# The first image's attention biases: interpolation along x moved from VectorE and ScalarE to TensorE, with diagonals made by GpSimd

## The chip, the cores and the metric

The kernel runs on one core of a Trainium2 chip. The core's engines work side by side, each through its own list of instructions in order: TensorE (PE in the profile; PEld is its weight loading), VectorE (DVE), ScalarE (ACT), GpSimd (POOL) and SyncE (SP, which here only starts transfers). The metric is the device time of one execution in microseconds (us). The kernel before takes 4742.62 us in the median of three runs (4736.29 to 4742.63).

## The reference, cut to what matters

The program takes four images of 32 x 32 positions with 384 channels through four residual layers. The change is in layer 0, a deformable attention with 6 heads of 64 channels. Its core is, per image:

```
offset = tanh(...) * [Hq/2, Wq/2];  pos = offset + ref          # one position per key and head
k, v  = projections of x sampled bilinearly at pos
attn  = einsum('bhmn', qh, k) * scale                           # 1024 queries x 1024 keys per head
disp  = (ref[query] - pos[key]) * 0.5
bias  = bilinear_sample(rpe_table[head], disp)                  # one value per (query, key)
attn  = softmax(attn + bias, over keys)
out   = attn @ v
```

For a fixed key the displacements of all queries form a regular grid, shifted by the key's own position. So the 1024 biases of one key are a window of a (doubled) table, read at one fractional shift in y and one in x. The kernel gathers such a window for each key and interpolates it twice: between neighbouring rows (y), and then between neighbouring columns (x). The weights of both steps belong to the key, so with keys on partitions they are one number per partition.

All of it is in 32-bit floats.

## The kernel before, in words

`kernel` builds the program image by image. Layer 0 of image 0 (`Front.layer0(0)`) runs to its end before the trunk (layers 1 to 3) of image 0 begins; the layer 0 of images 1 to 3 is woven into the trunk of the image before. So only in image 0 does layer 0's attention stand by itself. It has its own routine, `heads0`; images 1 to 3 use `head0`, which the change leaves alone.

`heads0` works in blocks (h, q, j): head h (6), half q of the queries (2), tile j of 128 keys (8), 96 blocks in all. A block's logits are 128 keys (partitions) x 512 queries. Eight blocks with the same h and q are called a half here; there are 12. One call of `turn(t)` issues one step of a software pipeline that is written out by hand, with `pin` keeping the order as written on every engine. With `AHEAD, SUB, OUT = 5, 10, 11`, turn t issues, for different blocks:

- POOL: the gather of the window `win` for block t+10 (L913, ring of 6 buffers);
- DVE: the second half of the y step for block i = t+5, `z = win_below * f + z` (L925), and the second half of the x step for block t+4, `lg = z_right * f + lg` (L930);
- ACT: the first half of the x step for block t+5, `lg = z_left * f` (L935), and the first half of the y step for block t+6, `z = win * f` (L944, `z` in a ring of 4);
- PE, in even turns: the products of keys and queries for blocks t+2 and t+3, into the two halves of one PSUM tile `big` (L955; there are two such tiles);
- DVE: `lg = product + lg` for block t (L975), and the running maximum over the key tiles, `rmax` (L980);
- at the end of a half, PE transposes `rmax` (L985), DVE reduces it (L966), POOL makes a diagonal of the maxima (L970), PE spreads it over all partitions by a product with ones (L1010), and ACT copies it to `tb` (L989);
- for block t-10: DVE subtracts `tb` (L994) and ACT takes the exponential (L995);
- for block t-11: PE multiplies by the values and, in the other half of its columns, by ones for the denominators (L1004, both accumulate over the eight blocks);
- after a half, ACT copies the outputs over the queries in `qpad` (L1019) and the row of denominators to a buffer (L1024) that SP sends to DRAM; `divide` fetches reciprocals back and scales the outputs (L905).

`lg` is a ring of 20 buffers of 128 x 512; two of them serve `divide` as `inv` from time to time. Beside the turns, `early0` (norm of image 1: transposes L560 and L583, group sums L338, their copies on ACT and statistics on DVE) is advanced by one step per turn. After the last turn comes the output projection (L388), which needs the scaled outputs of the last heads.

In PSUM, a block's result comes from two recorded passes of one product: the 96 products of L955 are 192 records.

Of the kernel before, what the change touches and what calls it, by code (L numbers as in the profile page):

```python
# [21 lines left out]
ALU = mybir.AluOpType  # L22
# [388 lines left out]
class Front(Lane):  # L411
# [447 lines left out]
    def heads0(self, work):  # L859

        nc, v, pin = self.nc, self.nc.vector, self.tc.keep_in_program_order
        f, va = self.f, self.va
        HH, HN = HW // 2, N // 2
# [1 line left out]
        blocks = [(h, q, j) for h in range(G) for q in range(2) for j in range(NJ)]  # L867
        n = len(blocks)

        AHEAD, SUB, OUT = 5, 10, 11  # L870
        win, z, lg, ps, half, dens, inv = {}, {}, {}, {}, {}, {}, {}

        def tile_of(shape, tag, bufs):
            return work.tile(shape, F32, tag=tag, name=self.nm(tag), bufs=bufs)
# [8 lines left out]
        def divide(step, k):  # L883
            heads = (2 * k, 2 * k + 1)
            by_row = lambda a: a.rearrange("o (p i) -> (o p) i", p=P)
            if step == 0:
                dens[k] = tile_of([P, 2, NJ], "dens", 2)
                for r, h in enumerate(heads):
                    nc.sync.dma_start(dens[k][:, r, :], by_row(self.den[h]))
            elif step == 1:  # L890
                pin(v.reciprocal(dens[k], dens[k]))
                for r, h in enumerate(heads):
                    nc.sync.dma_start(by_row(self.rden[h]), dens[k][:, r, :])
                for q in range(2):
                    inv[q] = tile_of([P, HN], "lg", 20)
                    for r, h in enumerate(heads):
                        nc.sync.dma_start(
                            inv[q][r * GC : (r + 1) * GC],
                            self.rden[h][0, q * HN : (q + 1) * HN].partition_broadcast(GC),
                        )  # L900
            else:
                for q in range(2):
                    out = queries(2 * k, q)
                    w = inv[q].rearrange("p (y x) -> p y x", x=HW)
                    pin(v.tensor_tensor(out, out, w, ALU.mult))  # L905

        def turn(t):
            i = t + AHEAD

            if i + 5 < n:  # L910
                h, q, j = blocks[i + 5]
                win[i + 5] = tile_of([P, (HH + 1) * WROW], "win", 6)
                nc.gpsimd.indirect_dma_start(  # L913
                    out=win[i + 5],
                    out_offset=None,
                    in_=self.strips[:, :],
                    in_offset=bass.IndirectOffsetOnAxis(
                        ap=self.widx[:, q, j * G + h : j * G + h + 1], axis=0
                    ),
                )  # L920
            at = lambda i: blocks[i][2] * G + blocks[i][0]
            sc = lambda i, axis, side: f[:, side, axis, at(i) : at(i) + 1]
            if 0 <= i < n:
                wv = win.pop(i).rearrange("p (r c) -> p r c", c=WROW)
                pin(v.scalar_tensor_tensor(  # L925
                    z[i], wv[:, 1 : HH + 1, 0 : HW + 1], sc(i, 1, 0), z[i], ALU.mult, ALU.add
                ))
            if 0 <= i - 1 < n:
                zi, lf = z.pop(i - 1), lg[i - 1].rearrange("p (y x) -> p y x", x=HW)
                pin(v.scalar_tensor_tensor(  # L930
                    lf, zi[:, :, 1 : HW + 1], sc(i - 1, 0, 0), lf, ALU.mult, ALU.add
                ))
            if 0 <= i < n:
                lg[i] = tile_of([P, HN], "lg", 20)
                pin(nc.scalar.activation(  # L935
                    lg[i].rearrange("p (y x) -> p y x", x=HW),
                    z[i][:, :, 0:HW],
                    AF.Copy,
                    scale=sc(i, 0, 1),
                ))  # L940
            if 0 <= i + 1 < n:
                wv = win[i + 1].rearrange("p (r c) -> p r c", c=WROW)
                z[i + 1] = tile_of([P, HH, HW + 1], "z", 4)
                pin(nc.scalar.activation(  # L944
                    z[i + 1], wv[:, 0:HH, 0 : HW + 1], AF.Copy, scale=sc(i + 1, 1, 1)
                ))

            if t >= -2 and (t + 2) % 16 == 0 and t + 18 < n and t + 2 >= 16:
                self.load_keys(blocks[t + 18][0])
            if t >= -2 and t % 2 == 0 and t + 2 < n:  # L950
                big = self.big()
                for u in range(2):
                    h, q, j = blocks[t + 2 + u]
                    ps[t + 2 + u] = big[:, u * 512 : (u + 1) * 512]
                    pin(nc.tensor.matmul(  # L955
                        ps[t + 2 + u],
                        self.kz[h % 2][:, j * P : (j + 1) * P],
                        queries(h, q),
                        start=True,
                        stop=True,  # L960
                    ))

            m = (t - 1) // NJ
            if t > 0 and t % NJ == 0 and t <= n:
                top = tile_of([P, NI], "top", 2)
                pin(v.tensor_reduce(  # L966
                    top, half[m, "t"].rearrange("p (i n) -> p i n", i=NI), AX.X, ALU.max
                ))
                diag = tile_of([P, NI, P], "diag", 1)
                pin(nc.gpsimd.tensor_tensor(  # L970
                    diag, bc(self.ident, 1, NI), bc(top, 2, P), ALU.mult
                ))
            if 0 <= t < n:
                m, j = divmod(t, NJ)
                pin(v.tensor_tensor(lg[t], ps.pop(t), lg[t], ALU.add))  # L975
                if j == 0:
                    half[m] = tile_of([P, HN], "rmax", 2)
                else:
                    first = lg[t - 1] if j == 1 else half[m]
                    pin(v.tensor_tensor(half[m], first, lg[t], ALU.max))  # L980
                if j == NJ - 1:
                    half[m, "t"] = self.bank()
                    for i in range(NI):
                        cols = slice(i * P, (i + 1) * P)
                        pin(nc.tensor.transpose(half[m, "t"][:, cols], half[m][:, cols], self.ident))  # L985
            if t > 1 and t % NJ == 1 and t <= n + 1:
                m = (t - 2) // NJ
                half[m, "b"] = tile_of([P, HN], "tb", 2)
                pin(nc.scalar.copy(half[m, "b"], half[m, "p"]))  # L989

            s = t - SUB
            if 0 <= s < n:
                tb = half[s // NJ, "b"]
                pin(v.tensor_tensor(lg[s], lg[s], tb, ALU.subtract))  # L994
                pin(nc.scalar.activation(lg[s], lg[s], AF.Exp))  # L995

            o = t - OUT
            if 0 <= o < n:
                h, q, j = blocks[o]
                if j == 0:  # L1000
                    half[o // NJ, "o"] = self.bank()
                po = half[o // NJ, "o"]
                for own, w in ((True, va[:, j, h * GC : (h + 1) * GC]), (False, self.ones[:, 0:GC])):
                    pin(nc.tensor.matmul(  # L1004
                        po[rows(h, own), :], w, lg[o], start=j == 0, stop=j == NJ - 1
                    ))
            if t > 0 and t % NJ == 0 and t <= n:
                m = (t - 1) // NJ
                half[m, "p"] = self.bank()
                pin(nc.tensor.matmul(  # L1010
                    half[m, "p"], self.ones, diag.rearrange("p i n -> p (i n)"),
                    start=True, stop=True,
                ))

            o = t - OUT - 1
            if 0 <= o < n and o % NJ == NJ - 1:
                h, q, j = blocks[o]
                po, own = half[o // NJ, "o"], rows(h, True)
                pin(nc.scalar.copy(  # L1019
                    queries(h, q)[own], po[own, :].rearrange("p (y x) -> p y x", y=HH)  # L1020
                ))
                o0 = rows(h, False).start
                den = lg[o][o0 : o0 + 1, :]
                pin(nc.scalar.copy(den, po[o0 : o0 + 1, :]))  # L1024
                nc.sync.dma_start(self.den[h][:, q * HN : (q + 1) * HN], den)

            o = t - OUT - 2
            for step, late in enumerate((0, 4, 9)):
                if o >= late and (o - late) % (4 * NJ) == 4 * NJ - 1:
                    divide(step, (o - late) // (4 * NJ))  # L1030
# [818 lines left out]
```

## Time and profile before

| | |
|---|---|
| median of the runs shown | 4742.62 us (4736.29 to 4742.63) |
| the profiled execution: its own time | 4731.65 us |
| the profiled execution: span of its instructions | 4729.8 us |
| mean granted TensorE clock | 0.926 |
| PE busy, of the whole span | 4165.4 us (88%) |
| DVE, ACT, POOL busy | 3133.8, 2416.1, 945.7 us |
| the stage of `heads0`: from the first product of keys and queries to the end of the last product with the values | 214.7 to 557.5 us of the span |

The page gives shares over the whole span, which has stages with different limits. For this change the stage from 214.7 to 557.5 us counts, and it is read with the same views limited to that window: busy time of each engine in stretches, groups of instructions by line, and the instructions in order of time. In a group, the number after x counts instructions, then come the busy time together (us) and the mean duration of one (ns); after the second bar stands how long the engine had been idle before them and what ended that. PE records overlap each other (a pass starts before the one ahead of it has drained), so a pass is priced by the distance between starts, not by its duration.

### The profile page before, as it was taken

To read this page: it belongs to the slowest core of one execution; us is meant where nothing else is said; L and a number is where in the kernel's file an instruction comes from. 1 tells how busy PE (TensorE), PEld (TensorE's weight loads), DVE (VectorE), ACT (ScalarE), POOL (GpSimd) and SP (SyncE) were. 2 spreads that over 40 slices of the span, in tenths; PEclk is the share of its full clock that TensorE was granted. 3 is DMA by queue.
4 is the path that set the end of the run, shared out by engine and by line. 5 is a ranking of instruction groups with operands and counts; after the bars stand their busy time and mean duration, and the time that the engine had idled before them with its cause. 6 is when DMAs were issued, how large, how long until landed. Compare 5 with 4: busy or idle time off the path is not lost. (4 is left out here: it accounts for less than half of the span.)

```text
span 4729.8 us, 46690 instructions
## 1 busy us (share of the span) xinstructions
PE 4165.4 (88%) x15704; PEld 1776.1 (38%) x15704; DVE 3133.8 (66%) x5772; ACT 2416.1 (51%) x3711; POOL 945.7 (20%) x946
## 2 busy tenths in 40 slices
PE   5477788999999988899899989899999999999988
PEld 2222233333333353333333444343333335343444
DVE  3599755777878727577877754767686874555544
ACT  2166433666666313566766332456675641556542
POOL 0533204221212103311212110421121211000000
PEclk8688888999999988999999989899999998999998
DMA  6435224221212143321212124431121213311011
GB/s 124 133 118 144 75 92 126 88 61 52 72 41 66 65 137 128 109 60 48 82 50 68 46 88 126 138 100 57 30 77 43 74 41 118 96 32 24 19 40 40
DMA packets 231727, 369.97 MB, mean 78 GB/s; under 512 B 117507, under 2 KB 164704, under 8 KB 231488
## 3 DMA queue, kind: packets, MB, share of 16 engines
q1 hardware_dynamic: 170472, 200.51, 14.3%
q0 software_dynamic: 39936, 145.53, 10.1%
q10 hardware_dynamic: 21080, 20.96, 1.8%
q8 instruction: 124, 2.03, 0.2%
q14 instruction: 115, 0.94, 0.1%
HBM read 287.41 MB, written 79.78 MB: 78 GB/s over the span
## 5 line engine op out<-in xcount | busy, mean ns | idle before, releaser
L1472 DVE SCALAR_TENSOR_TENSOR e<-bank,gam,e 128x512 f32<-128x512 f32 x768 | 558.4, 749 | 573.0 <-ACT gn L1471 276.8
L1463 PE MATMUL bank<-whole,sg 128*128 128x512 f32 (+3 forms) x2304 | 873.2, 513 | 2.5 <-DVE e L1472 2.5
L1323 ACT ACTIVATE big<-big,nmax 128x1024 f32<-128x1024 f32 x384 | 418.6, 1090 | 397.5 <-DVE nmax L1322 352.0
L1441 ACT ACTIVATE e<-big 128x1024 f32<-128x1024 f32 x384 | 376.9, 1019 | 360.4 <-PE big L1433 352.8
L1463 PEld LDWEIGHTS bank<-whole,sg 128*128 128x128 f32 x2304 | 406.5, 199 | 379.9 <-issue 301.7
L1322 DVE TENSOR_REDUCE nmax<-big 128x1 f32<-128x1024 f32 x384 | 453.0, 1218 | 62.0 <-PE big L1314 35.4
L792 POOL DMA_INDIRECT win<-strips,widx x288 | 307.1, 1066 | 634.0 <-DVE z L805 331.0
L1418 POOL TENSOR_SCALAR sg<-whole,gam 128x512 f32<-128x512 f32 x192 | 147.1, 769 | 1399.4 <-PE bank L1463 1139.5
L1433 PE MATMUL big<-qa,ka 64*128 64x512 f32 x1536 | 411.7, 627 | 14.7 <-ACT big L1323 8.9
L1314 PE MATMUL big<-k,q 32*128 32x512 f32 x1536 | 327.2, 690 | 74.7 <-ACT e L1441 35.3
L813 PE MATMUL bank<-qpad,kz 128*128 128x512 f32 x576 | 281.1, 614 | 15.0 <-DVE e L1472 15.0
L707 POOL DMA_INDIRECT gat<-pairs,sidx x192 | 210.0, 1094 | 418.0 <-DVE sidx L521 241.2
L848 PE MATMUL bank<-lg,va 128*64 128x512 f32 x576 | 265.4, 603 | 16.3 <-ACT lg L846 16.2
L848 PE MATMUL bank<-lg,ones 128*64 128x512 f32 x576 | 264.7, 602 | 0.0
L810 DVE SCALAR_TENSOR_TENSOR lg<-z,bias_f,lg 128x512 f32<-128x512 f32 x288 | 227.4, 802 | 39.3 <-ACT lg L809 37.1
L804 ACT ACTIVATE z<-win,bias_f 128x528 f32<-128x528 f32 x288 | 207.1, 739 | 63.1 <-DVE lg L810 40.0
L1433 PEld LDWEIGHTS big<-qa,ka 64*128 64x128 f32 x1536 | 134.7, 187 | 270.4 <-issue 153.9
L805 DVE SCALAR_TENSOR_TENSOR z<-win,bias_f,z 128x528 f32<-128x528 f32 x288 | 217.0, 772 | 27.4 <-DMA win<-strips,widx 16.4
L845 DVE TENSOR_TENSOR lg<-lg,tb 128x512 f32<-128x512 f32 x288 | 187.7, 705 | 52.3 <-ACT tb L838 51.5
L1407 PE MATMUL bank<-e,vs 128*32 128x512 f32 x1536 | 211.6, 607 | 2.1 <-DVE vs L1401 2.1
L809 ACT ACTIVATE lg<-z,bias_f 128x512 f32<-128x512 f32 x288 | 201.0, 720 | 18.3 <-PE bank L848 10.4
L814 DVE TENSOR_TENSOR lg<-bank,lg 128x512 f32<-128x512 f32 x288 | 192.4, 684 | 20.7 <-PE bank L813 18.4
(299 smaller groups left out, 6658.3 us busy)
## 6 DMA issues: line engine op xcount, KB each, us to landing
pairs<-xn SPq DMA_DIRECT2D x64, 192.0 KB
q<-qd SPq DMA_DIRECT2D x48, 256.0 KB
w<-in_gmat SPq DMA_DIRECT2D x16, 576.0 KB
w<-in_w_off SPq DMA_DIRECT2D x12, 576.0 KB
w<-in_Wqkv SPq DMA_DIRECT2D x12, 576.0 KB
a<-in_x SPq DMA_DIRECT2D x16, 384.0 KB
x<-a ACTq DMA_DIRECT2D x4, 1536.0 KB
win<-strips,widx POOLq DMA_INDIRECT x384
```

The source lines that it names most:

```text
L792: nc.gpsimd.indirect_dma_start(out=win, out_offset=None, in_=self.strips[:, :], in_offset=bass.IndirectOffsetOnAxis(ap=self.widx[:, q, c : ...
L805: v.scalar_tensor_tensor(z, wv[:, 1 : HH + 1, 0 : HW + 1], sc(0, 1), z, ALU.mult, ALU.add)
L810: v.scalar_tensor_tensor(lg, z[:, :, 1 : HW + 1], sc(0, 0), lg, ALU.mult, ALU.add)
L813: nc.tensor.matmul(ps, kz[:, j * P : (j + 1) * P], both, start=True, stop=True)
L848: nc.tensor.matmul(po[out, :], w, lf, start=j == 0, stop=j == NJ - 1)
L1314: nc.tensor.matmul(ps[r][:, h * 512 : (h + 1) * 512], self.q4[rows, i * P : (i + 1) * P], self.k4[rows, 0:512], start=True, stop=True,)
L1322: v.tensor_reduce(nmax[:, r, i : i + 1], ps[r], AX.X, ALU.max, negate=True)
L1323: nc.scalar.activation(ps[r], ps[r], AF.Exp, bias=nmax[:, r, i : i + 1], accum_out=den[:, r, i : i + 1],)
L1433: nc.tensor.matmul(ps[:, r, :], ka[rows, j * P : (j + 1) * P], qa[rows, cols], start=True, stop=True,)
L1441: nc.scalar.activation(e, ps, AF.Exp)
L1463: nc.tensor.matmul(ps[:, (mid - i0) * P :], sg[:, r, m, :], sim[:, r, m, mid * P : i1 * P], start=m == 0, stop=m == 1,)
L1472: v.scalar_tensor_tensor(e[:, r, :], ps, self.gam[:, 1:2], e[:, r, :], ALU.add, ALU.mult, accum_out=tot[:, r, h : h + 1],)
```

## The change

In `heads0` alone, the x step and the addition of the logits leave DVE and ACT:

- L930 (x step, second half), L935 (x step, first half) and L975 (adding the product) are gone.
- POOL makes, for each block, `dg`: the identity times the key's two x weights, two diagonals of 128 x 128 side by side (ring of 5).
- PE makes a block's logits in PSUM from three products in place of one: diagonal times left columns of `z`, diagonal times right columns of `z`, keys times queries.
- ACT copies the finished logits from PSUM to `lg`; DVE takes the running maximum directly from PSUM.
- `z` has 7 buffers in place of 4, `lg` 15 in place of 20, and the denominators' row is put in the half's `tb` in place of an `lg` buffer.

```diff
-        AHEAD, SUB, OUT = 5, 10, 11
+        AHEAD, SUB, OUT, LG = 5, 10, 11, 15
...
-            if 0 <= i - 1 < n:
-                zi, lf = z.pop(i - 1), lg[i - 1].rearrange("p (y x) -> p y x", x=HW)
-                pin(v.scalar_tensor_tensor(
-                    lf, zi[:, :, 1 : HW + 1], sc(i - 1, 0, 0), lf, ALU.mult, ALU.add
-                ))
             if 0 <= i < n:
-                lg[i] = tile_of([P, HN], "lg", 20)
-                pin(nc.scalar.activation(
-                    lg[i].rearrange("p (y x) -> p y x", x=HW),
-                    z[i][:, :, 0:HW],
-                    AF.Copy,
-                    scale=sc(i, 0, 1),
+                dg[i] = tile_of([P, 2, P], "dg", 5)
+                pin(nc.gpsimd.tensor_tensor(
+                    dg[i],
+                    bc(self.ident, 1, 2),
+                    bc(f[:, :, 0, at(i) : at(i) + 1].rearrange("p s o -> p (s o)"), 2, P),
+                    ALU.mult,
                 ))
...
-                z[i + 1] = tile_of([P, HH, HW + 1], "z", 4)
+                z[i + 1] = tile_of([P, HH, HW + 1], "z", 7)
...
-                    pin(nc.tensor.matmul(
-                        ps[t + 2 + u],
-                        self.kz[h % 2][:, j * P : (j + 1) * P],
-                        queries(h, q),
-                        start=True,
-                        stop=True,
-                    ))
+                    zi, di = z.pop(t + 2 + u), dg.pop(t + 2 + u)
+                    terms = (
+                        (di[:, 1, :], zi[:, :, 0:HW]),
+                        (di[:, 0, :], zi[:, :, 1 : HW + 1]),
+                        (self.kz[h % 2][:, j * P : (j + 1) * P], queries(h, q)),
+                    )
+                    for k, (w, a) in enumerate(terms):
+                        pin(nc.tensor.matmul(ps[t + 2 + u], w, a, start=k == 0, stop=k == 2))
...
-                pin(v.tensor_tensor(lg[t], ps.pop(t), lg[t], ALU.add))
+                lg[t] = tile_of([P, HN], "lg", LG)
+                pin(nc.scalar.copy(lg[t], ps[t]))
...
-                    pin(v.tensor_tensor(half[m], first, lg[t], ALU.max))
+                    pin(v.tensor_tensor(half[m], first, ps[t], ALU.max))
...
-                den = lg[o][o0 : o0 + 1, :]
+                den = half[o // NJ, "b"][o0 : o0 + 1, :]
```

More of the change, by code (lines that the diff above doesn't have):

```diff
@@ L868, in heads0 @@
         n = len(blocks)
-        AHEAD, SUB, OUT = 5, 10, 11
-        win, z, lg, ps, half, dens, inv = {}, {}, {}, {}, {}, {}, {}
+        AHEAD, SUB, OUT, LG = 5, 10, 11, 15
+        win, z, dg, lg, ps, half, dens, inv = {}, {}, {}, {}, {}, {}, {}, {}
         def tile_of(shape, tag, bufs):
@@ L894, in divide @@
                 for q in range(2):
-                    inv[q] = tile_of([P, HN], "lg", 20)
+                    inv[q] = tile_of([P, HN], "lg", LG)
                     for r, h in enumerate(heads):
```

## The prediction

> **What bounds the kernel now.** I looked first for the place of the changed lines: the groups by line put all of L913 to L1024 between 183 and 558 us. Nothing else of weight stands beside this stage, as the next one cannot begin without its outputs, so what it gains or loses the whole time does. Next I took the busy time of each engine in that window, in three plain halves of it, and in three later stretches where PE is dense. Columns: length, then busy us (instructions) of PE, PEld, DVE, ACT and POOL, granted clock, DMA share, GB/s.
>
> ```profile
> 214.70:557.50 342.80, 260.11 (x732) 84.78 (x730) 325.25 (x501) 212.86 (x337) 119.79 (x100) 0.85 0.39 117
> 415.70:442.40 26.70, 21.12 (x59) 6.22 (x56) 26.46 (x41) 17.30 (x28) 10.79 (x10) 0.88 0.34 104
> 442.40:469.10 26.70, 19.36 (x52) 5.75 (x54) 26.46 (x42) 17.51 (x28) 10.79 (x10) 0.89 0.31 95
> 600.00:700.00 100.00, 95.71 (x410) 39.63 (x410) 51.88 (x85) 33.18 (x50) 0.00 (x0) 0.96 0.25 76
> 1200.00:1400.00 200.00, 190.49 (x768) 75.64 (x765) 148.10 (x284) 125.24 (x202) 34.53 (x37) 0.97 0.16 49
> 4400.00:4500.00 100.00, 94.69 (x442) 40.34 (x441) 56.45 (x130) 60.68 (x93) 6.89 (x10) 1.00 0.09 23
> ```
>
> DVE is busy for 26.46 of a half's 26.70 us: it bounds the stage. But PE is second, at 21 of 27 us, and its figure is swollen by a clock of 0.85. DVE in order of time shows one turn:
>
> ```profile
> 447.52 0.69 DVE L994 TENSOR_TENSOR lg<-lg,tb 128x512 f32<-128x512 f32 x1
> 448.12 0.77 DVE L925 SCALAR_TENSOR_TENSOR z<-win,bias_f,z 128x528 f32<-128x528 f32 x1
> 448.80 0.75 DVE L930 SCALAR_TENSOR_TENSOR lg<-z,bias_f,lg 128x512 f32<-128x512 f32 x1
> 449.46 0.69 DVE L975 TENSOR_TENSOR lg<-big,lg 128x512 f32<-128x512 f32 x1
> 450.19 0.69 DVE L980 TENSOR_TENSOR rmax<-rmax,lg 128x512 f32<-128x512 f32 x1
> 450.79 0.68 DVE L994 TENSOR_TENSOR lg<-lg,tb 128x512 f32<-128x512 f32 x1
> ```
>
> From L994 to L994 are 3.27 us without a gap; eight turns and the reduction (0.6) make the 26.7. The change adds work to PE, so its prices come from PE in order of time, where it runs without a stop:
>
> ```profile
> 440.69 0.63 PE L985 MATMUL bank<-ident,rmax 128*128 128x128 f32 x4 [3.05 <-DVE rmax L980]
> 441.25 0.64 PE L1004 MATMUL bank<-lg,va 128*64 128x512 f32 x1
> ...
> 442.26 1.99 PE L955 MATMUL big<-qpad,kz 128*128 128x512 f32 x4
> 444.18 0.64 PE L1004 MATMUL bank<-lg,va 128*64 128x512 f32 x1
> ...
> 445.19 1.13 PE L1010 MATMUL bank<-diag,ones 128*128 128x512 f32 x2
> 446.24 0.64 PE L1004 MATMUL bank<-lg,va 128*64 128x512 f32 x1
> ...
> 658.63 5.32 PE L388 MATMUL big<-whole,w 128*128 128x512 f32 x12
> 663.78 1.02 PE L1160 MATMUL bank<-whole,w 128*128 128x512 f32 x2
> ```
>
> Twelve passes of 512 columns take 658.63 to 663.78, 5.15 us: 0.43 each. A group between others of another shape costs 0.20 more (L955: 442.26 to 444.18 is 1.92, four passes are 1.72). A block's products with the values take 1.01 us (441.25 to 442.26; the two column halves run together), two blocks in a row 4 x 0.43 + 0.15 = 1.87. The transposes take 0.56, the product with ones 1.05.
>
> **The change part by part.** *DVE.* L930 and L975 go: by starts 0.66 and 0.73 us a turn, so a turn falls to 1.9 and a half to 15.8 us. The maximum now reads PSUM; L975, which does so, has 683 ns against L980's 690: nothing. What is new is POOL beside it: while the present diagonal L970 runs, L994 takes 1.33 us at 443.60 instead of 0.69. If each `dg` costs DVE its whole length, 0.55 us, a half is 20.2.
>
> *ACT.* L935 (722 ns) goes, a copy from PSUM comes; L989 is the same copy, 586 ns. A half falls from 17.4 to about 16.3 us.
>
> *POOL.* Gather 1.21 us a block as now, and `dg`, 128 x 256. L970 is the same operation at twice the size, 1.08 us, so 0.55 by size; 1.42, the longest L970, is the upper end. A half is 8 x 1.76 + 1.08 = 15.2 us, at the upper end 22.1.
>
> *PE.* Two blocks now need 12 passes in one group, 12 x 0.43 + 0.20 = 5.36 us, and 1.87 for the values: 7.23. A half is 4 x 7.23, transposes 0.56, ones 1.05 and 0.15 for the values' group that the transposes split: 30.7 us. That is more than the 26.7 that a half takes now, and more than any other engine's new half. **PE becomes the bound.**
>
> *The stage's sum on PE.* 48 pairs x 7.23 = 347.0; 12 half ends x 1.76 = 21.1; the other PE work of the window (L560 4.2, L583 4.2, L388 3.8, L338 2.8 and 1.6, L402 0.5) 17.1. Together 385.2 us against the present 342.8: **+42.4**. Added: 2 us at the end, when PE has only two blocks' values left while the last `tb`, subtraction and exponential pass (0.58 + 0.68 + 0.63), and 2 us for some passes below full clock. **+46 us.**
>
> *Which clock.* This is the largest doubt, since the stage's own row says 0.85, the dense stretches 0.96 to 1.00. At 0.85 the sum would be 385.2 / 0.85 = 453, +110. I take the dense rows, because the new stage is dense: its start (L402, back to back until 214.7) already is, and no wait of PE is left in a half. The Trainium skill ("TensorE: Matmul & The Clock Gate", Part 1) has the gate the same way round: the array runs at half rate after an idle window of about 3.4 us and at full rate while kept busy. By it the sum is 385 and the 0.85 is the price of today's waits, such as the 3.05 us before L985 above.
>
> *Waits that the change adds.* A filling of `big` now waits for `z` (DVE), `dg` (POOL), and for maximum and copy of the blocks that held the buffer (DVE and ACT, formerly DVE alone); behind it on PE are the values' products. From the moment a pair's logits stand, DVE needs 0.6 + 0.6 + 0.7 + 0.6 and a `dg`'s 0.55 until the second maximum, about 3.1 us; PE meanwhile does values, the other buffer's filling and values, 9.1 us. That leaves 6 us. `z` is made three turns ahead. `dg` of block t+5 waits on POOL until PE has read block t's; behind it is the next gather, then due four turns later, 14.5 us (now 13.1), and no wait on a gather shows in this stage. The skill ("SBUF — State Buffer", two separate sides) speaks against giving POOL this work: a DVE operation with two SBUF inputs and a POOL operation exclude each other for their whole length. L994's 1.33 agrees. By it DVE's half is the 20.2 above, without it 15.8; neither is the bound.
>
> *What costs nothing, and its cover.* The present waits of L955 on L1019 (12.9 us on PE) vanish, as the diagonals' products come first in a filling; they lie under DVE now. Rings: an `lg` buffer is read by PE two to four turns before its reuse, ahead in PE's own order. The denominators' row in `tb` must be sent before the next-but-one half's copy, six turns or 22 us later; the transfers of this row and back at 557.5 to 563 take 2 us each. If those covers fail, a turn is lost, about 4 us per half or 48.
>
> **The rivals.** *PE waits, or stays off full clock* (+62 to +110): PE at 0.93 gives 414, +73 with the end; at 0.85 +110; a wait of 3 us per half, +36 more. For it: today's 0.85. Against: six us of slack at every filling.
>
> *PE near its floor* (+10 to +30): no 0.2 for a change of group and other work absorbed: 48 x 16 x 0.43 + 12 x 1.61 + 13 = 362.6, +20. For it: L388's even 0.43. Against: every change of shape in the lines above shows the extra.
>
> *Faster*: DVE stays the bound and its half of 15.8 to 20.2 counts, at most 12 x (26.7 - 20.2), 78 us less. The place is the filling: PE's half must be under 26.7, so (26.7 - 1.76 - 1.4) / 64 = 0.37 us a pass. No row shows less than 0.42. *No change to measure* (within 10 us) needs 0.39.
>
> *POOL the bound*: for 30.7 us a half, each `dg` would have to take 2.5 us, more than twice L970 at double the size; I count it under the first.
>
> **How the numbers follow.** PE dense, +30 to +62: 0.66. Waits or clock: 0.16. Floor: 0.11. Within 0.2% (9.5 us, about what a measurement can tell from no change): 0.03. Faster: 0.04. So faster 0.04, same 0.03, slower 0.93. The profiled execution would go from 4731.65 to about 4778. It ran 11 us under the median of the runs, which I take as the base: 4742.62 + 46, **4788 us**. The range goes from +20 (the floor) to +80 (clock near 0.91): 4762 to 4823.
>
> **What the new profile would show.** The reductions at the half ends stand 30 to 31.5 us apart in place of 26.7. In a half PE is busy nearly throughout with a clock of 0.95 or more, and DVE falls to 16 to 20 us. Fillings start 5.4 us before the next group, and the waits before them are gone. The maxima and the copies wait for PE. L994 and L925 often take over 1 us, beside `dg`. The prediction is wrong if fillings wait for `dg`, if the clock stays at 0.85, or if passes stand closer than 0.43.

## The result, and the profile after

The changed kernel takes 4780.97 us (median of four runs, 4778.16 to 4782.36) against 4739.45 (4736.17 to 4742.63): a ratio of 1.0090 with a 95% interval of 1.0077 to 1.0103, 41.5 us slower. The forecast was +46, at 4788. The profiled execution took 4779.59 us, its span is 4777.8.

The view of busy time in stretches, for the stage (first filling of `big` to the end of the last product with the values) and for two plain halves in it. Columns: length, busy us (instructions) of PE, PEld, DVE, ACT, POOL, granted clock, DMA share, GB/s.

```profile
217.30:598.80 381.50, 379.39 (x1116) 144.87 (x1115) 225.22 (x310) 192.36 (x335) 180.22 (x193) 1.00 0.35 105
434.80:465.60 30.80, 30.80 (x88) 11.24 (x88) 18.77 (x24) 15.69 (x28) 18.34 (x19) 1.00 0.38 106
465.60:496.40 30.80, 30.80 (x88) 11.23 (x88) 19.61 (x24) 15.76 (x28) 15.56 (x17) 1.00 0.28 82
```

PE is busy for 379.39 of 381.50 us at a clock of 1.00; in the two halves it never stops. DVE fell from 26.46 to 19 us a half. A half takes 30.80 us where it took 26.70. The stage is 38.7 us longer (381.5 against 342.8) and in this execution began 2.6 us later; what follows it took 4179.1 us in place of 4172.4, which is taken for the scatter between executions, since the same code stands there (the second profile of the changed kernel, in experiment 7, has 4174.1).

PE in order of time, one pair of blocks:

```profile
458.49 1.98 PE L958 MATMUL big<-z,dg 128*128 128x512 f32 x4
460.31 1.02 PE L958 MATMUL big<-qpad,kz 128*128 128x512 f32 x2
461.17 1.88 PE L958 MATMUL big<-z,dg 128*128 128x512 f32 x4
```

Four passes with the diagonals take 458.49 to 460.31, 1.82 us with the 0.1 of a group's start, two with the keys 0.86 (460.31 to 461.17): 0.43 a pass, strided `z` or not.

Groups by line in the stage (count | busy us, mean ns | idle before it and what ended that), first two of the kernel before, then those of the changed one:

```profile
L955 PE MATMUL big<-qpad,kz 128*128 128x512 f32 x192 | 118.0, 747 | 25.8 <-ACT qpad L1019 12.9 <-DVE lg L975 12.7
L925 DVE SCALAR_TENSOR_TENSOR z<-win,bias_f,z 128x528 f32<-128x528 f32 x94 | 72.0, 766 | 3.1 <-ACT z L944 3.1
```

```profile
L958 PE MATMUL big<-z,dg 128*128 128x512 f32 x384 | 183.8, 601 | 0.0
L958 PE MATMUL big<-qpad,kz 128*128 128x512 f32 x192 | 98.1, 592 | 0.0
L931 POOL TENSOR_TENSOR dg<-ident,bias_f 128x256 f32<-128x256 f32 x93 | 73.1, 786 | 7.7 <-PE big L958 6.0
L926 DVE SCALAR_TENSOR_TENSOR z<-win,bias_f,z 128x528 f32<-128x528 f32 x94 | 92.4, 986 | 6.5 <-ACT z L940 6.5
L978 DVE TENSOR_TENSOR rmax<-rmax,big 128x512 f32<-128x512 f32 x72 | 49.3, 685 | 110.9 <-ACT lg L973 110.9
```

No filling waits (0.0 idle before either group). The products with the keys, 747 ns each before, are down to 592, since no pass of a filling runs below full clock (none takes over 0.70 us). The y step on DVE grew from 766 to 986 ns beside GpSimd's diagonals, and a diagonal took 786 ns where 550 had been taken. The last line is one that nobody expected: the maximum waits for ScalarE's copy of the same block, 110.9 us in all. Both only read `big` (but for the second block of a half, whose maximum takes the copy too), so by the data alone most maxima need not wait; why the program orders them so was not tested.

### The profile page after: what moved, and what is told of

It is laid out like the page before. It is cut to its first block, busy times and chain, and to the rows that moved or that the text cites. A ratio compares the mean times of both kernels' runs of the same rounds, so it can differ in the third digit from the quotient of the medians.

```text
span 4777.8 us, 47383 instructions
## 1 busy us (share of the span) xinstructions
PE 4283.8 (90%) x16088; PEld 1835.1 (38%) x16088; DVE 3032.5 (63%) x5580; ACT 2396.5 (50%) x3711; POOL 1012.7 (21%) x1042
## 5 line engine op out<-in xcount | busy, mean ns | idle before, releaser
L848 PE MATMUL bank<-lg,va 128*64 128x512 f32 x576 | 266.5, 605 | 16.3 <-ACT lg L846 16.2
L809 ACT ACTIVATE lg<-z,bias_f 128x512 f32<-128x512 f32 x288 | 201.2, 720 | 19.6 <-PE bank L848 11.4
```

Of the source, the lines that this page charges most:

```text
L848: nc.tensor.matmul(po[out, :], w, lf, start=j == 0, stop=j == NJ - 1)
```

## The experiments

The experiments were timed in three sets, each on another chip and each with the kernel before beside it: 1 to 4, 5 and 6, 7 and 8. The kernel before took about 4700 us in the first two and 4742 in the third, so the totals that the expectations name must be read as differences from it, and the stage's length in each trace says the rest. The part behind the stage took 4128 to 4141 us in the profiles of the first two sets and 4172 to 4185 in the others, so the 40 us between the chips lie outside the stage, and stages may be compared across sets. (In the edits shown, the `stop` flag, which moves to the last product of the group, is left out.)

**1. One diagonal product left out.** Is the stage only PE's passes, or does something stand right behind PE?

```diff
                     terms = (
-                        (di[:, 1, :], zi[:, :, 0:HW]),
                         (di[:, 0, :], zi[:, :, 1 : HW + 1]),
...
```

> Kernel: the changed one, without the product of the left columns (their share of the biases is left out); diagonals, copies and maxima stay. A filling has 8 passes in place of 12: 8 x 0.43 + 0.20 = 3.64 us, a half 30.81 - 4 x 1.72 = 23.9 us. Theory PE alone (the stage is the sum of PE's passes): the stage loses 48 x 1.72 = 82.6 us, total 4781 - 83 = 4698 us, PE idle under 10 us in the stage, clock 1.00. Rival, the chain behind PE (in the trace of after the maximum waits for ACT's copy of the same block, the exponential for the subtraction, and the next copy stands 3.1 to 3.3 us after the last): 8 x 3.2 + half end 1 = 26.6 us a half, total 4781 - 12 x 4.2 = 4730 us, DVE and PE both with waits, clock below 1.00.

Measured: 0.9985 of the kernel before (0.9974 to 0.9995), 8 us faster than it; so some 50 us less than the changed kernel and not 83. Halves are 27.1 to 27.7 us where they are plain. The rival's 26.6 was near, PE alone (23.9) was not. The stage of this kernel:

```profile
215.60:552.50 336.90, 304.44 (x924) 108.06 (x922) 218.85 (x310) 190.87 (x335) 181.53 (x193) 0.99 0.39 119
```

No engine is full: PE is busy for 304.44 of 336.90 us. ACT in order of time shows the loop:

```profile
455.12 0.56 ACT L972 COPY lg<-big 128x512 f32<-128x512 f32 x1
457.26 0.63 ACT L992 ACTIVATE lg<-lg 128x512 f32<-128x512 f32 x1 [1.57 <-DVE lg L991]
457.79 0.72 ACT L940 ACTIVATE z<-win,bias_f 128x528 f32<-128x528 f32 x1
458.42 0.56 ACT L972 COPY lg<-big 128x512 f32<-128x512 f32 x1
460.56 0.63 ACT L992 ACTIVATE lg<-lg 128x512 f32<-128x512 f32 x1 [1.57 <-DVE lg L991]
```

From copy to copy are 3.30 us. DVE, in the same stretch, shows what ACT waits for:

```profile
455.72 0.69 DVE L977 TENSOR_TENSOR rmax<-rmax,big 128x512 f32<-128x512 f32 x1 [0.76 <-ACT lg L972]
456.32 0.90 DVE L991 TENSOR_TENSOR lg<-lg,tb 128x512 f32<-128x512 f32 x1
457.14 1.12 DVE L926 SCALAR_TENSOR_TENSOR z<-win,bias_f,z 128x528 f32<-128x528 f32 x1
```

Copy, then maximum, then subtraction, then exponential, then the y step's first half, then the next copy: five operations on two engines in one ring.

**2. GpSimd's diagonals taken away.** The first five blocks' diagonals serve all blocks.

```diff
+                if i >= 5:
+                    dg[i] = dg[i - 5]
+                else:
+                    ... (the diagonal as in the changed kernel)
```

> Kernel: the changed one, but GpSimd makes the diagonals of the first five blocks only and all later blocks use those again (their own weights are left out). Theory PE: time as the changed kernel's, 4781 within 6 us, halves 30.8 us; the y step on VectorE falls from 986 ns to about 770, which nobody sees. Rival, VectorE and GpSimd in each other's way take part in the bound: 96 x 0.2 = 20 us or more less, 4761 or below.

Measured: 1.0075 of the kernel before (1.0055 to 1.0095), a stage of 384.7 us with plain halves of 30.81:

```profile
215.70:600.40 384.70, 382.73 (x1116) 146.48 (x1114) 206.14 (x310) 192.35 (x335) 107.19 (x102) 0.99 0.34 104
```

The y step on DVE fell to 849 ns, less than expected but by 137 ns, and nothing came of it. (81 of its 94 instructions have no GpSimd operation on tensors beside them and take 760 ns in the mean; 11 start while GpSimd makes the diagonal of the maxima at a half's end, L970, and take 1459.) GpSimd and its effect on DVE are no part of the price of the change.

**3. One diagonal product more.**

```diff
                         (di[:, 0, :], zi[:, :, 1 : HW + 1]),
+                        (di[:, 0, :], zi[:, :, 1 : HW + 1]),
...
```

> Kernel: the changed one with the product of the right columns issued twice (biases wrong by that share), 16 passes a filling in place of 12. Theory PE: 96 x 2 x 0.43 = 82.6 us more, 4864 us, halves 30.81 + 6.88 = 37.7 us, clock 1.00. Rival, PE's time is partly waiting on other engines that the longer filling would cover: clearly less, 40 to 60 us more.

Measured: 1.0260 (1.0240 to 1.0281), 121.6 us over the kernel before and so 80 over the changed one's 41.5; in the traces the stage is 465.7 us, 84.2 more, and plain halves are 37.68. Each further pass costs its full 0.43 us: (37.68 - 30.81) / 16 = 0.43. The whole stage, 84.2 / 192 = 0.44, has a little more in it, and that little lies in one stretch of one half (the stage, that stretch, and the passes in it):

```profile
215.30:681.00 465.70, 465.12 (x1308) 183.12 (x1306) 221.54 (x310) 193.57 (x335) 177.96 (x193) 0.99 0.28 86
376.70:382.00 5.30, 5.30 (x7) 2.21 (x8) 4.53 (x8) 3.48 (x6) 2.23 (x3) 0.50 0.82 283
376.75 5.44 PE L959 MATMUL big<-z,dg 128*128 128x512 f32 x6
```

Six passes stand 0.88 us apart there, at a clock of 0.50, although PE has had no gap. Just ahead of them, from 371.87 to 376.75, run two groups of 14 products with one column each (L338), a block's products with the values between them. Experiment 2 has such a stretch behind the same products (a clock of 0.90 from 345 to 379 us), and in both the half with it is 3.3 us longer than the next; the changed kernel has the products and no such stretch. What decides was not tested.

**4. The kernel before, plus diagonals that nobody reads.** What does GpSimd beside a full DVE cost?

```diff
+                dg = tile_of([P, 2, P], "dg", 3)
+                pin(nc.gpsimd.tensor_tensor(
+                    dg,
+                    bc(self.ident, 1, 2),
+                    bc(f[:, :, 0, at(i) : at(i) + 1].rearrange("p s o -> p (s o)"), 2, P),
+                    ALU.mult,
+                ))
```

> Kernel: the one before, plus GpSimd making each block's two diagonals (ring of 3), which nobody reads. VectorE is the bound here, so this prices what a diagonal costs VectorE. If GpSimd holds VectorE up for the diagonal's whole length by size (0.55 us): 96 x 0.55 = 53 us more, 4792 us. If only as much as the y step lengthened in the changed kernel (0.22 us): 21 us more, 4760 us. If not at all: 4739 us.

Measured: 1.0095 (1.0078 to 1.0111), 43 us more, between the 53 of the first expectation and the 21 of the second; the stage is 384.8 us, 42.0 more, a plain half 30.68 instead of 26.69: 0.50 us of DVE for each block. The stage:

```profile
214.30:599.10 384.80, 274.31 (x732) 88.66 (x730) 368.54 (x501) 214.53 (x337) 208.16 (x193) 0.81 0.35 104
```

DVE's groups show which operations pay, first two of the kernel before, then three of this one:

```profile
L994 DVE TENSOR_TENSOR lg<-lg,tb 128x512 f32<-128x512 f32 x96 | 72.2, 758 | 1.3 <-ACT tb L989 1.3
L975 DVE TENSOR_TENSOR lg<-big,lg 128x512 f32<-128x512 f32 x96 | 65.5, 683 | 0.0
```

```profile
L1001 DVE TENSOR_TENSOR lg<-lg,tb 128x512 f32<-128x512 f32 x96 | 101.1, 1060 | 1.3 <-ACT tb L996 1.3
L925 DVE SCALAR_TENSOR_TENSOR z<-win,bias_f,z 128x528 f32<-128x528 f32 x94 | 77.1, 820 | 1.6 <-ACT z L951 1.6
L982 DVE TENSOR_TENSOR lg<-big,lg 128x512 f32<-128x512 f32 x96 | 65.0, 677 | 1.0 <-PE big L962 1.0
```

L1001 is the subtraction (L994 before, 758 ns), L982 the addition that reads PSUM (L975 before, 683 ns): the first is slowed by 302 ns, the other not at all. For the addition this row proves little, though: in the trace the subtraction ran beside a block's diagonal 67 times of 96 (1210 ns in the mean), the addition once. Whether an operand in PSUM protects an operation is seen in other runs, in the last section.

**5. One diagonal, made by GpSimd.** A middle way that all of this points to: half of the added passes, and one DVE operation in the place of two.

```diff
-                    zi, di = z.pop(t + 2 + u), dg.pop(t + 2 + u)
+                    zi, di = z[t + 2 + u], dg.pop(t + 2 + u)
                     terms = (
-                        (di[:, 1, :], zi[:, :, 0:HW]),
-                        (di[:, 0, :], zi[:, :, 1 : HW + 1]),
+                        (di, zi[:, :, 0:HW]),
...
-                pin(nc.scalar.copy(lg[t], ps[t]))
+                by_y = lambda x: x.rearrange("p (y x) -> p y x", x=HW)
+                pin(v.scalar_tensor_tensor(
+                    by_y(lg[t]), z.pop(t)[:, :, 1 : HW + 1], sc(t, 0, 0), by_y(ps[t]),
+                    ALU.mult, ALU.add,
+                ))
...
-                    pin(v.tensor_tensor(half[m], first, ps[t], ALU.max))
+                    pin(v.tensor_tensor(half[m], first, lg[t], ALU.max))
```

(`dg` is then one diagonal of the left weight, and `z` has 8 buffers.)

> Kernel: a middle way. GpSimd makes one diagonal (left weight), TensorE adds its product and the logits in PSUM, VectorE adds the right columns in one operation that reads PSUM and writes the logits; ScalarE has neither the x step nor a copy. PE: 8 passes a filling, half 23.9 us. VectorE: 0.68 + 0.68 + 0.65 + 0.6 a turn and the reduction, 21.5 us a half, plus GpSimd in the way, 8 x 0.3 = 24. Theory, the larger of both: 24 us a half against 26.7 before, 12 x 2.8 = 33 us less than before, 4706 us. Rival, waits between the two (both nearly full): 27 us a half, no gain, 4740.

Measured: 0.9942 of the kernel before (0.9926 to 0.9959), 30 us faster; plain halves 25.0 to 25.3 us, between the 24 of the theory and the 27 of the rival.

**6. One diagonal, made by ScalarE.** The edit is shown against experiment 5.

```diff
-                pin(nc.gpsimd.tensor_tensor(
-                    dg[i], self.ident, f[:, 1, 0, at(i) : at(i) + 1].broadcast_to([P, P]),
-                    ALU.mult,
-                ))
+                pin(nc.scalar.activation(dg[i], self.ident, AF.Copy, scale=sc(i, 0, 1)))
```

> Kernel: as the middle way with one diagonal on TensorE, but ScalarE makes the diagonal (identity times the weight) in place of GpSimd. ScalarE then has the y step 0.73, the diagonal about 0.3 and the exponential 0.63 a turn, 14 us a half with the copies. VectorE 21.5 us a half with no GpSimd in the way. Theory: PE's 23.9 us a half, 4781 - 83 = 4698 us, 40 less than before. If GpSimd was not in the way, no difference to the version with GpSimd's diagonal.

Measured: 0.9918 of the kernel before (0.9901 to 0.9934), 42.6 us faster, as the theory had it. Plain halves are 23.6 to 24.5 us, and the stage 306.7 us against 322.0 with GpSimd's diagonal. The stages of experiments 5 and 6:

```profile
214.20:536.20 322.00, 303.92 (x924) 109.41 (x922) 298.48 (x406) 145.30 (x238) 157.30 (x193) 0.98 0.41 124
```

```profile
215.10:521.80 306.70, 299.66 (x924) 108.44 (x922) 270.13 (x406) 172.90 (x331) 99.14 (x100) 0.99 0.43 131
```

With GpSimd's diagonal PE and DVE are both near full (303.92 and 298.48 of 322); without it DVE is busy for 28 us less and PE is the bound again, 299.66 of 306.70. This version beats both kernels, each compared with the kernel before in its own set.

**7. The changed kernel once more**, beside the kernel before in the third set.

> Kernel: the changed one itself, beside the kernel before on the chip of the other experiments, whose kernel before takes about 4700 us and not 4740. Theory PE: what the change costs is the stage's length, 381.5 - 342.8 = 38.7 us and the 2.6 us by which it begins later, so 41 us here too, halves 30.8 us. If part of the difference came from outside the stage or from the chip, it is not 36 to 46 us.

Measured: 1.0089 (1.0071 to 1.0107), 38.4 us more, stage 381.5 us, plain halves 30.81. The set landed where the kernel before takes 4742 us, so it repeats the first comparison, and does not carry it to the chips of the first two sets; there experiment 2 has the same plain halves of 30.81.

**8. The ring of experiment 1 opened.** ScalarE takes the exponential one turn after the subtraction.

```diff
-        AHEAD, SUB, OUT, LG = 5, 10, 11, 15
+        AHEAD, SUB, OUT, LG = 5, 10, 12, 15
...
-                pin(nc.scalar.activation(lg[s], lg[s], AF.Exp))
+            if 0 <= s - 1 < n:
+                pin(nc.scalar.activation(lg[s - 1], lg[s - 1], AF.Exp))
```

> Kernel: the one with a single diagonal product (left share missing), with ScalarE's exponential of a block, and with it TensorE's product with the values, one turn later, so that ScalarE's next copy no longer stands behind a subtraction of the same turn. Theory chain (copy, maximum, subtraction, exponential, y step, next copy held the halves at 27.3 us): halves fall to 24 to 25 us, the stage from 337 to about 305 us, TensorE's idle time in it from 32.5 to under 15 us. Rival, something else holds the halves (the gathers, VectorE with GpSimd's diagonals in the way): they stay at 26.5 us or more.

Measured: 0.9946 of the kernel before (0.9926 to 0.9966), where experiment 1 had 0.9985. The stage is 314.2 us in place of 336.9, PE idle for 14.6 us in it. Four of the last halves stand at 24.66, 23.94, 23.94 and 26.84 us. ACT in order of time, where PE holds it now:

```profile
456.40 0.56 ACT L972 COPY lg<-big 128x512 f32<-128x512 f32 x1
456.86 0.62 ACT L993 ACTIVATE lg<-lg 128x512 f32<-128x512 f32 x1
457.39 0.72 ACT L940 ACTIVATE z<-win,bias_f 128x528 f32<-128x528 f32 x1
458.35 0.59 ACT L972 COPY lg<-big 128x512 f32<-128x512 f32 x1 [0.23 <-PE big L957]
```

A copy follows the last after 1.95 us, not 3.30. The ring was the bound of experiment 1. Opening it took 22.7 us off a stage in which PE had idled for 32.5. Of the 305 expected, PE's own 299.6 leave 5.4 us for waits, and 14.6 were found; that makes the nine us between 305 and 314.2. The halves over 26.5 us are of two kinds. The third to the fifth interval between reductions (28.25, 26.97 and 26.99 us) carry the norm of image 1, which makes the same intervals of the changed kernel 3 to 4 us longer than its plain ones. The other two (27.47 and 26.84) hold waits of PE, 1.58 us the longest: the filling at 486.28 waits for a maximum, the maximum for ScalarE's copy at 484.82, and that copy stands in ScalarE's order behind the copies of a finished half's outputs and denominators (482.86 and 483.46).

## Why the prediction was right, point by point

**The bound moves from DVE to PE.** Right. PE was to be the longest engine with 30.7 us a half; it is 30.81, without idle time. Experiment 3 shows the slope (0.43 us a pass in plain halves), and experiment 2 that GpSimd and what it does to DVE had no share.

**The pass at 0.43 us**, read off a dense stretch of another stage. Right: it holds for weights that GpSimd has just made and for a strided moving operand.

**The stage's sum.** 385.2 and 4 us were forecast, 381.5 found. The halves fit (30.81 against 30.68). Read in the trace by the distance between starts, the products of the halves take 366.7 us (368.1 forecast), the other PE work 12.6 (17.1 forecast), and PE is idle for 2.1 (4 allowed). So the other work was mis-sized, and its price, not the clock, is the reason: at a clock of 1.00 the same groups still show 16.2 us of busy time (L560 and L583 4.3 each), because records overlap their neighbours. The prediction priced its passes by starts, and these groups by busy time. Of the 4 us allowed, the end took 0.5 (a wait of 480 ns before the last L1008), a wait for the maximum in one of the halves with the norm of image 1 took 1.5, and the clock nothing. The stage thus ended 7.7 us under its forecast, the median only 4.5 (41.5 against 46), because the kernels differ by 2.8 us more than their stages do. No run shows where these 2.8 us come from; that much of the closeness is luck.

**Which clock.** Right to take the dense rows: 1.00 in the stage, no pass of a filling over 0.70 us where before the passes of L955 averaged 747 ns. The Trainium skill's gate ("TensorE: Matmul & The Clock Gate", Part 1) says the same, that an array kept busy runs at the full rate. In experiment 1 PE idles 32.5 us in pieces, one of them over 3 us (3.23), and the clock still is 0.99; in the kernel before it idles 82.7 us, with 11 pieces over 3 us, at 0.85; in experiment 4 110.5 us, with 15 such pieces, at 0.81. The page's measure is an idle window of about 3.4 us; here the sum and the number of long pieces rise together, and the runs do not tell which counts. Nor is a PE without gaps always at full clock: experiments 2 and 3 have the stretch at half clock shown there, 3.3 us each. The 2 us set aside for slow passes were not needed in the changed kernel, and would have been too few in those two.

**DVE's half, 15.8 to 20.2.** Right, 18.8 and 19.6. That a diagonal costs DVE 0.55 us was a fair price: 0.50 in the plain halves of experiment 4, where DVE is the bound. It is not quite the diagonal's whole length, as one that met nothing took 0.62 to 0.63 us (experiments 2 and 8). And it was mostly the y step that paid (986 ns for 766); the subtraction took 747 ns (758 before) and was not often over 1 us.

**POOL, 0.55 us a diagonal.** Too low: 786 ns in the mean, and 926 beside a full DVE, inside the stated ends of 0.55 and 1.42. GpSimd's half of 15.6 to 18.3 us is still far from 30.8.

**The slack of 6 us at every filling.** Wrong in its working, without effect here. It took DVE's operations one after another and ACT as free. In the program the maximum waits for ACT's copy of its block, and ACT's next copy waits, through exponential and subtraction, for the maximum. This ring takes 3.1 to 3.3 us a turn, some 27.3 us a half in experiment 1. Below PE's 30.8 that leaves 3.5 us in a half, not 6 in a filling: the rival "PE waits" was closer than the text made it. And one step further the same mistake would have counted: by the prediction's own terms, taking off one product should have given 23.9 us a half, and gave 27.3.

**The rivals.** *Faster* fell with its condition, a pass under 0.37 us. *Near the floor* fell too: a half of 64 x 0.43 + 1.61 = 29.1 us stood against the 30.81 found, so the group changes cost what had been read. *PE waits, or stays off full clock* fell with 2.1 us of idle time at a clock of 1.00. *POOL the bound* was excluded by experiment 2.

## What to carry to other kernels

Before work is moved from a full engine to one that looks three quarters busy, price it on the receiver by the distance between starts in a dense stretch, and compare half with half: here each of the two added products takes 16 passes of 0.43 us of TensorE in a half, 6.9 us, and each VectorE operation that goes gives back about 0.69 x 8 = 5.5 us. Moving half of it (experiment 6, with ScalarE making the diagonal) took 43 us off where moving all of it put 41 on. And of engines that are not the bound, follow the ring of waits, not only the busy time: the next bound after PE was no engine but five operations that wait for each other.

## What the runs showed of the hardware that had not been expected

A VectorE operation that takes one operand from PSUM is not held up by GpSimd. In the changed kernel the maximum, which reads PSUM, started 12 times while a GpSimd operation on tensors was running and never took over 689 ns (685 in the mean of all); the y step, with two operands in SBUF, started so 39 times and took 1186 ns in the mean, against 761 with no such operation beside it. In experiment 5 the sum from PSUM started 8 times beside a running one and took 739 ns (741 in the mean of experiment 6, without GpSimd's diagonals), while the maximum, there with both operands in SBUF, went to 830 from 692 in experiment 6, and in experiment 4 the subtraction from 758 to 1060. The page "SBUF — State Buffer" of the Trainium skill (two separate sides) names two inputs in SBUF as the condition, and these rows agree. GpSimd pays as well: its 128 x 256 diagonal took 786 ns in the changed kernel, 744 ns where DVE had more room (experiment 3) and 926 ns beside a full DVE (experiment 4).

A PE that shows no gap is not always at full clock: behind 28 products of one column, passes stood 0.88 us apart at a clock of 0.50 in experiment 3, and not in the changed kernel, which has the same products.

ScalarE makes a 128 x 128 diagonal in 392 ns, though it had been taken for 300, and VectorE is not held up by it: in experiment 6 the subtraction takes 755 ns and the y step 764 (758 and 766 in the kernel before).
